# A graph layer with a routed feed-forward network: two first-layer blocks in one PSUM bank, ScalarE's copies and the result sums later in the order, and a new list of expert steps

## Chip, cores and metric

The kernel runs on one core of a Trainium2 chip. The metric is the device time of one execution in microseconds. The profile is of one further execution on the same kind of core.

## What is computed

6250 nodes have 256 features each. There are 106,250 edges (50,000 random pairs in both directions, and a loop at each node), sorted by their destination.

```python
deg = maximum(number of edges into each node, 1);  norm = deg ** -0.5
h   = layernorm(x) @ W.T + b                       # 256 -> 256
x   = x + norm * segment_sum((norm * h)[src], dst) # 6250 nodes
n   = layernorm(x)
s   = n @ Wg.T + bg                                # 8 experts
the two best experts of each node, weights p = softmax(their scores)
x   = x + sum over both: p * (relu(n @ W1[e].T + b1[e]) @ W2[e].T + b2[e])   # 256 -> 1024 -> 256
```

## The kernel before

**Preparation.** A first part (`in_order`, up to line 320) counts the edges of each node, normalises the rows and writes them as a table to HBM, each as two float16 halves.

**Chunks.** The edges are cut into 831 chunks of 128. The main loop (line 840) runs over the chunks as slots `s`. In each slot GpSimd gathers the 128 source rows of a chunk by an indirect DMA, six slots ahead (`gather`, line 387, into 24 `rows` buffers), VectorE makes a 0/1 matrix of destinations (`mask`), and one matmul on TensorE adds the rows up by destination (`add_up`, line 399) in a PSUM tile `ps`. A window of destinations closes every few chunks: `join` (line 470) adds the high and low halves on VectorE into `rolled`, and ScalarE copies 32 to 96 rows of it into `whole`, the sums of a tile of 128 nodes (line 486).

**Node tiles.** There are 49. `FINAL[t]` is the last chunk that adds to tile t. From the slot after it on, a fixed order of small parts follows: `turn_sum` transposes the sums, `linear` multiplies by W and Wg, `route` (one part in each slot) does the layer norm, picks the two experts, finds each row's place in its experts' queues (a small matmul "rank", `pp`), sorts the rows by expert through `sort` (matmuls with a 0/1 matrix) and `send` writes them by eight DMAs into the queues in HBM (`hq`, from `ordered`). ScalarE takes part with copies out of PSUM and the exponential `ex`.

**Expert steps.** A step takes up to 256 rows (or 128) of one expert's queue, the fullest one, which the chip itself finds (`choose`). `load_first`, `load_rows` and `load_second` issue the DMAs of W1, of the rows `xT` and of W2 on SP's queue. The arithmetic of a step is cut into pieces. `up(step, b)` (line 722) is one first-layer block: 128 of the 1024 hidden units, four float32 matmul instructions into a PSUM tile `ph`, then a Relu by ScalarE into `hid` (line 732). There are eight. `down(step, i)` (line 734) is two of the eight parts of the second layer for 128 rows: four matmul instructions into `py`; after every fourth piece VectorE adds the bias (`y`, line 744) and SP writes 128 rows to `yq`. A step of 256 rows has 8 + 8 pieces, one of 128 rows 8 + 4.

**The order around the change.** All of it is written out in Python; each engine runs its instructions in that order. `tasks[s]` has what a slot runs beside its chunk. Steps follow tiles: one step for each tile from tile 3 on, two for tiles 42, 44 and 46 (`FOLLOWS`). `fetch` (choice and loads) starts 14 slots after the tile's last chunk, the first piece 14 slots later (`earliest`). Each slot runs one piece, and a second in every fourth slot when the next step is due too (lines 848 to 850). In the slots behind the last chunk (`ftail`) one piece runs in each slot, steps are chosen and loaded as they are used up, and the results are read back by indirect DMAs (`read_back`), added to x by VectorE (`add_in`) and stored. There are 56 steps: 49 from the list and 7 behind it, the last four of 128 rows, so 13,824 rows. `DONE` lists pairs of a step and a number of tiles: once that step is done the results of so many tiles are taken to be there. If the chip finds that one was not, or another assumption failed, it sets `bad` and runs a second, general program (`any_order`).

[...] `ps`, `ph` and `py` have two buffers each, `pt` and `px` one.

Of the kernel before, what the change touches and what calls it, by code (L numbers as in the profile page):

```python
# [7 lines left out]
F32 = mybir.dt.float32  # L8
# [11 lines left out]
P = 128  # L20
N = 6250
NT = 49
# [14 lines left out]
SLOTS = 64  # L37
FIRST_STEP = 3
EXTRA = (42, 44, 46)
FOLLOWS = [t for t in range(FIRST_STEP, NT) for _ in range(1 + (t in EXTRA))]  # L40
USUAL = len(FOLLOWS) + 7
SHORT = 4
W1C = 2 * H + HB
# [14 lines left out]

DONE = ((40, 29), (42, 33), (43, 34), (44, 35), (45, 36), (46, 38), (47, 39), (48, 40), (49, 41), (50, 42),
        (51, 44), (52, 45), (53, 46), (54, 47), (USUAL - 1, NT))  # L60
LATER = 1 << 17
# [71 lines left out]
def in_order(ctx: ExitStack, tc: tile.TileContext, g: Shared):  # L133
# [7 lines left out]

    yq = dram.tile([P + USUAL * FT, D], F32, name="fyq")

# [207 lines left out]
    for step, t1 in DONE:  # L351
        nc.vector.memset(bounds[:, t0:t1, :], float(P + (step + 1) * FT))
        t0 = t1
# [19 lines left out]
    nc.vector.memset(most, 0.0)  # L373

    zero = keep.tile([P, FT * D // P], F32, name="zero")
    nc.gpsimd.memset(zero, 0.0)  # L376

# [5 lines left out]
    def free_order(ins, others, why):  # L383
        for o in others:
            tc.declare_no_dep(ins.ins, o.ins, reason=why)
# [63 lines left out]

    def clear_results():  # L450

        for step in range(USUAL - SHORT, USUAL):
            r0 = P + step * FT + P
            nc.sync.dma_start(yq[r0:r0 + FT - P, :], zero[:, :D])

    kept = {w: (WINDOWS[w - 1][0] % P, WINDOWS[w][0] - WINDOWS[w - 1][0]) for w in range(1, len(WINDOWS))}
    keeps = {}
    for j, key in enumerate(sorted(set(kept.values()))):  # L460
        keeps[key] = keep.tile([P, 1], F32, name=f"keep{j}")
        nc.gpsimd.memset(keeps[key], 1.0)  # L462
        for t, p0, p1 in pieces(key[0], key[0] + key[1]):
            nc.gpsimd.memset(keeps[key][p0:p1, :], 0.0)
    whole, turned_sums, turned_inputs = {}, {}, {}

# [3 lines left out]
    def join(w):  # L470

        nonlocal rolled
        n0 = WINDOWS[w][0]
        n1 = WINDOWS[w + 1][0] if w + 1 < len(WINDOWS) else NP
        ps = sums.pop(w)
        new = work.tile([P, D], F32, name="rolled", bufs=3)
        if w:
            nc.vector.scalar_tensor_tensor(new, rolled, keeps[kept[w]], ps[:, 0:D], op0=OP.mult, op1=OP.add)  # L478
        else:
            nc.vector.tensor_copy(new, ps[:, 0:D])  # L480
        nc.vector.tensor_add(new, ps[:, D:2 * D], new)  # L481
        rolled = new
        for t, p0, p1 in pieces(n0, n1):
            if p0 == 0:
                whole[t] = work.tile([P, D], F32, name="whole")
            nc.scalar.activation(whole[t][p0:p1, :], new[p0:p1, :], AF.Copy)  # L486
# [158 lines left out]

    def rows_of(step):
        return P if USUAL - SHORT <= step < USUAL else FT

    def choose(step):
        n = rows_of(step)  # L650
        seen = placed
# [32 lines left out]
        to = work.tile([P, 1], F32, name="to")  # L684
        nc.vector.tensor_scalar(to, of[:, 0:1], -1.0, float(P + step * FT - LATER), op0=OP.mult, op1=OP.add)
        mine = work.tile([P, NT, 2], F32, name="mine")
# [10 lines left out]
    def load_rows(step):  # L697

        f = steps[step]
        assert sent >= f["known"]  # L700
        col = nc.values_load(f["go"][0:1, 1:2], engines=(SP,), min_val=0, max_val=CAP - FT)
        f["xT"] = work.tile([P, FT, 2], F32, name="xT", bufs=4)
        n = rows_of(step)
        nc.sync.dma_start(f["xT"][:, :n, :], hq[bass.ds(f["we"], P), bass.ds(col, n), :])
# [6 lines left out]
    def fetch(step):  # L711

        for _ in choose(step):
            yield
            if step in steps and "w1" not in steps[step]:
                load_first(step)
        while sent < steps[step]["known"]:
            yield
        load_rows(step)
        load_second(step)  # L720

    def up(step, b):
        f = steps[step]
        w1 = f["w1"]
        n = rows_of(step)
        if b == 0:
            f["hid"] = work.tile([P, HB, FT], F32, name="hid")
        ph = psp.tile([P, FT], F32, name="ph")
        for k in range(2):
            nc.tensor.matmul(ph[:, :n], w1[:, k * H + b * P:k * H + (b + 1) * P], f["xT"][:, :n, k],  # L730
                             start=(k == 0), stop=(k == 1))
        nc.scalar.activation(f["hid"][:, b, :n], ph[:, :n], AF.Relu, bias=w1[:, 2 * H + b:2 * H + b + 1])  # L732

    def down(step, i):
        f = steps[step]
        a = i // 4
        if i % 4 == 0:
            f["py"] = psp.tile([P, D], F32, name="py")
        for b in (2 * (i % 4), 2 * (i % 4) + 1):
            nc.tensor.matmul(f["py"], f["hid"][:, b, a * P:(a + 1) * P], f["w2"][:, b * D:(b + 1) * D],  # L740
                             start=(b == 0), stop=(b == HB - 1))
        if i % 4 == 3:
            y = work.tile([P, D], F32, name="y", bufs=4)
            nc.vector.tensor_add(y, f["py"], f["w2"][:, HB * D:])  # L744
            r0 = P + step * FT + a * P
            w = nc.sync.dma_start(yq[r0:r0 + P, :], y)
            free_order(w, reads, "results are written once, and read once written")
            writes.append((step, w))
        if i == 4 * rows_of(step) // P - 1:
            del steps[step]  # L750


# [16 lines left out]

    earliest = {}  # L770
    for t in range(NT):
        s = FINAL[t] + 1
        plan_at(s + 2, turn_sum, t)
        plan_at(s + 4, linear, t)
        in_parts(s + 5, route, t)
        s += LATE[t]
        for i, step in enumerate(k for k, tile in enumerate(FOLLOWS) if tile == t):
            in_parts(s + 14 + 4 * i, fetch, step)
            earliest[step] = s + 28 + 4 * i
    for w, (n0, chunks) in enumerate(WINDOWS):  # L780
        tasks.setdefault(chunks[-1] + 1, []).insert(0, (join, (w,)))
    plan_at(3, centre)
    for t in range(0, NT, 2):
        plan_at(4 + t // 2 * 3, inputs_turned, t, min(t + 2, NT))
        plan_at(6 + t // 2 * 3, inputs_scored, t, min(t + 2, NT))
    plan_at(30, clear_results)
    chosen = loaded1 = loaded2 = len(FOLLOWS)
    all_sent = FINAL[NT - 1] + 1 + 19

    cur = 0  # L790
    done = 0

# [4 lines left out]

    def read_back(pool, where, t, j, upto=USUAL - 1):
        yb = pool.tile([P, D], F32, name="yb", bufs=12)
        r = nc.gpsimd.indirect_dma_start(  # L800
            out=yb, out_offset=None, in_=yq[0:P + (upto + 1) * FT, :],
            in_offset=bass.IndirectOffsetOnAxis(ap=where[:, t, j:j + 1], axis=0))
        free_order(r, [w for step, w in writes if step > upto], "rows of later steps aren't read")
        reads.append(r)
        return t, j, yb
# [5 lines left out]
    def store(t0, t1, engine=None):  # L811
# [4 lines left out]
        if t1 == NT:  # L816
            engine.dma_start(g.out[(NT - 1) * P:N, :], g.xr[:LAST, NT - 1, :])

    def next_piece(s):

        nonlocal cur, done
        step = done
        if step >= USUAL or "xT" not in steps.get(step, {}) or s < earliest.get(step, 0):
            return
        if cur < HB:
            up(step, cur)
        else:
            down(step, cur - HB)
        cur += 1
        if cur == HB + 4 * rows_of(step) // P:  # L830
            done += 1
            cur = 0

    with tc.manual_schedule():
        with rowp as rowpool:
            for c in range(AHEAD):
                gather(c)
            for c in range(MASKS):
                mask(c)
            for s in range(NC):  # L840
                if s + AHEAD < NC:
                    gather(s + AHEAD)
                if s + MASKS < NC:
                    mask(s + MASKS)
                add_up(s)
                for fn, args in tasks.pop(s, []):
                    fn(*args)
                next_piece(s)
                if s % 4 == 0 and earliest.get(done + 1, NC) <= s:
                    next_piece(s)  # L850
        with tc.tile_pool(name="ftail", bufs=2) as pool:
# [16 lines left out]
            while done < USUAL or tasks or len(plan) > 1 or asked < 2 * allowed or pend:  # L868
                for fn, args in tasks.pop(s, []):
                    fn(*args)  # L870
                if s > all_sent:
                    if chosen < min(USUAL, done + 4):
                        run(choose(chosen))
                        chosen += 1
                    if loaded2 < min(loaded1, done + 3):
                        load_second(loaded2)
                        loaded2 += 1
# [8 lines left out]
                if len(plan) > 1 and done > plan[0][0] and s >= since.get(plan[0][0], 0) + 6 \  # L886
                        and asked == 2 * allowed:
                    step, t1 = plan.pop(0)
                    results(allowed, t1, float(P + (step + 1) * FT))
                    allowed = t1  # L890
# [10 lines left out]

            results(allowed, NT, float(P + USUAL * FT))
            late = work.tile([P, NT, 2], F32, name="late", bufs=1)
# [555 lines left out]
```

## Time and profile before

| | |
|---|---|
| median of 3 runs | 1585.66 us (1575.81, 1585.66, 1592.05) |
| profiled execution | 1341.47 us, its span 1339.7 us |
| mean granted TensorE clock in it | 0.956 |
| busy share: TensorE, VectorE, GpSimd, ScalarE | 88%, 74%, 67%, 30% |
| gathers (GpSimd, line 389) | 831, 953 ns each |
| first-layer matmuls (line 730) | 1792 |
| second-layer matmuls (line 740) | 1728 |
| Relu (line 732) | 448, 465 ns each |
| HBM | 269.01 MB read, 55.42 MB written |

The profile comes from one execution, which was shorter than the three timed ones. A group of instructions is named by its line, engine, and output and inputs; "idle before" is the time in which its engine did nothing before it, with what ended that wait. A matmul's recorded duration runs to the modelled end of its pipeline, so successive matmuls overlap in the record, and their starts tell the rate. "PEld" is the loading of weights into TensorE. SP's DMA issues and register loads are not counted as busy.

### The profile page before, as it was taken

The page shows a single profiled execution, that of the slowest core. Times are in us where ns is not written, and L with a number is a line of the kernel's source. Part 1 is how long each engine was busy: PE and PEld are TensorE (multiplying, and loading weights), DVE is VectorE, ACT ScalarE, POOL GpSimd, SP SyncE. Part 2 cuts the span into 40 slices and gives each one's busy share as a digit, 9 for nine tenths or more (in the row PEclk, how much of TensorE's full clock was granted, in tenths as well). Part 3 has the DMA queues.
Part 4 walks back from the last instruction along what each step waited for, and adds up shares of the span by engine and source line. Part 5 has one row for each costly group of instructions (what it writes and reads, how often), then busy time and mean ns, then how long its engine had stood idle before and what let it go on. Part 6 is the DMA issues. An engine that isn't in the chain of part 4 may idle for free.

```text
span 1339.7 us, 23956 instructions
## 1 busy us (share of the span) xinstructions
PE 1179.6 (88%) x6224; PEld 901.0 (67%) x6224; DVE 985.5 (74%) x5327; ACT 402.5 (30%) x931; POOL 903.7 (67%) x984
## 2 busy tenths in 40 slices
PE   4439895999899999999999999999999999889984
PEld 4417562777576677767777676776777777678873
DVE  8842657787888888888888888888877775765542
ACT  2622331232333233332323323233232222222221
POOL 2047777777777777777777777777777775347743
PEclk9999666999999999999999999999999999799987
DMA  8353456788787878788787888877978987679882
GB/s 297 112 160 104 122 138 193 227 282 272 230 250 261 274 239 286 239 268 265 251 289 228 279 258 254 288 240 270 296 229 280 296 305 236 230 235 338 313 314 89
DMA packets 158459, 326.16 MB, mean 243 GB/s; under 512 B 26708, under 2 KB 105256, under 8 KB 143976
## 3 DMA queue, kind: packets, MB, share of 16 engines
q1 hardware_dynamic: 110780, 194.17, 42.1%
q0 software_dynamic: 46864, 129.82, 33.2%
q8 instruction: 51, 0.84, 0.3%
q14 instruction: 96, 0.79, 0.2%
q10 hardware_dynamic: 668, 0.55, 0.1%
HBM read 269.01 MB, written 55.42 MB: 242 GB/s over the span
## 4 chain that ended last, share of the span: by engine, by line
PE 46%; DMA 23%; DVE 16%; issue 5%; SPq 5%; ACT 4%; POOL 2%; POOLq 0%; ACTq 0%; DVEq 0%
PE ph L730 18%; PE py L740 11%; DMA xT<-fhq 8%; PE ps L403 7%; DMA fhq<-ordered 6%; SPq L641 4%; DMA yb<-fyq,rowat 4%; DMA rows<-ftable,src 3%; PE ph L446 2%; PE pt L501 2%; PE px L629 2%; DVE mask L396 2%; DVE y L744 1%; POOL yb L800 1%; DVE rolled L481 1%
## 5 line engine op out<-in xcount | busy, mean ns | idle before, releaser
L389 POOL DMA_INDIRECT rows<-ftable,src x831 | 791.6, 953 | 253.1 <-issue 105.5
L730 PE MATMUL ph<-xT,w 128*128 128x256 f32 (+1 forms) x1792 | 472.4, 392 | 45.4 <-DMA xT<-fhq 35.7
L740 PE MATMUL py<-w,hid 128*128 128x256 f32 x1728 | 435.8, 382 | 3.9 <-DVE y L744 3.9
L730 PEld LDWEIGHTS ph<-xT,w 128*128 128x128 f32 x1792 | 322.5, 192 | 144.8 <-issue 46.6
L740 PEld LDWEIGHTS py<-w,hid 128*128 128x128 f32 x1728 | 329.8, 192 | 80.4 <-DVE y L744 4.1
L403 PE MATMUL ps<-rows,mask 128*128 128x512 f16 x831 | 318.6, 399 | 38.0 <-DMA fyq<-zero 29.9
L732 ACT ACTIVATE hid<-ph,w 128x256 f32<-128x256 f32 (+1 forms) x448 | 204.6, 465 | 291.5 <-PE ph L730 283.8
L396 DVE TENSOR_SCALAR mask<-col_b,rel 128x128 f16<-128x128 bf16 x831 | 210.0, 272 | 28.9 <-PE ps L403 28.8
L486 ACT ACTIVATE whole<-rolled 32x256 f32<-32x256 f32 (+2 forms) x156 | 64.6, 414 | 346.2 <-DVE rolled L481 345.5
L800 POOL DMA_INDIRECT yb<-fyq,rowat x98 | 94.1, 960 | 90.4 <-DVE mx L543 26.2
L403 PEld LDWEIGHTS <-mask 128*128 128x128 f16 x831 | 87.4, 105 | 67.3 <-POOL keep L462 26.1
L744 DVE TENSOR_TENSOR y<-py,w 128x256 f32<-128x256 f32 x108 | 45.4, 421 | 96.2 <-PE py L740 93.3
L478 DVE SCALAR_TENSOR_TENSOR rolled<-rolled,keep,ps 128x256 f32<-128x256 f32 x149 | 70.7, 474 | 18.0 <-PE ps L403 17.6
L808 DVE SCALAR_TENSOR_TENSOR xr<-yb,prob,xr 128x256 f32<-128x256 f32 x98 | 45.7, 482 | 50.7 <-DMA yb<-fyq,rowat 49.6
L481 DVE TENSOR_TENSOR rolled<-ps,rolled 128x256 f32<-128x256 f32 x150 | 63.6, 424 | 5.2
L501 PE MATMUL pt<-gw,uT 128*128 128x264 f32 x196 | 55.9, 411 | 2.0 <-DVE spot L595 2.0
L509 DVE SCALAR_TENSOR_TENSOR xr<-pt,norm,xr 128x256 f32<-128x256 f32 x49 | 23.7, 483 | 41.7 <-PE pt L501 41.5
L446 PEld LDWEIGHTS ph<-wg,turned 128*128 128x128 f32 x196 | 38.6, 289 | 16.8 <-ACT turned L438 16.1
L199 PE MATMUL count<-oh,ol 128*16 128x8 bf16 (+2 forms) x898 | 28.9, 174 | 22.2 <-DVE oh L188 17.9
L501 PEld LDWEIGHTS pt<-gw,uT 128*128 128x128 f32 x196 | 39.4, 203 | 13.5 <-DVE spot L595 2.1
L376 POOL MEMSET zero<- 128x512 f32 x1 | 0.5, 524 | 64.5 <-DMA ftable<-tab 64.5
L199 PEld LDWEIGHTS <-ol 128*16 128x16 bf16 x898 | 28.7, 109 | 22.5 <-DVE ol L185 16.2
(188 smaller groups left out, 1144.6 us busy)
## 6 DMA issues: line engine op xcount, KB each, us to landing
w<-in_W SPq DMA_DIRECT2D x56, 1152.0 KB
w<-in_W SPq DMA_DIRECT2D x56, 1028.0 KB
fhq<-ordered SPq DMA_DIRECT2D x392, 64.0 KB
fyq<-y SPq DMA_DIRECT2D x108, 128.0 KB
xT<-fhq SPq DMA_DIRECT2D x52, 256.0 KB
rows<-ftable,src POOLq DMA_INDIRECT x831
out<-xr POOLq DMA_DIRECT2D x11, 512.0 KB
xr<-in_x SPq DMA_DIRECT2D x6, 896.0 KB
```

The source lines that it names most:

```text
L389: nc.gpsimd.indirect_dma_start(out=rows[c], out_offset=None, in_=table[:, :], in_offset=bass.IndirectOffsetOnAxis(ap=g.src[:, c:c + 1], ax ...
L396: nc.vector.tensor_scalar(masks[c], g.col_b[:, r:r + P], g.rel[:, c:c + 1], None, op0=OP.is_equal)
L403: nc.tensor.matmul(sums[w], masks.pop(c), rows.pop(c), start=(c == chunks[0]), stop=(c == chunks[-1]))
L446: nc.tensor.matmul(px, xT[:, k, (t - t0) * P:(t - t0 + 1) * P], wg[:, k, :], start=(k == 0), stop=(k == 1))
L478: nc.vector.scalar_tensor_tensor(new, rolled, keeps[kept[w]], ps[:, 0:D], op0=OP.mult, op1=OP.add)
L481: nc.vector.tensor_add(new, ps[:, D:2 * D], new)
L486: nc.scalar.activation(whole[t][p0:p1, :], new[p0:p1, :], AF.Copy)
L501: nc.tensor.matmul(pl, uT[:, k, :], gw[:, k, :], start=(k == 0), stop=(k == 1))
L730: nc.tensor.matmul(ph[:, :n], w1[:, k * H + b * P:k * H + (b + 1) * P], f["xT"][:, :n, k], start=(k == 0), stop=(k == 1))
L732: nc.scalar.activation(f["hid"][:, b, :n], ph[:, :n], AF.Relu, bias=w1[:, 2 * H + b:2 * H + b + 1])
L740: nc.tensor.matmul(f["py"], f["hid"][:, b, a * P:(a + 1) * P], f["w2"][:, b * D:(b + 1) * D], start=(b == 0), stop=(b == HB - 1))
L800: r = nc.gpsimd.indirect_dma_start(out=yb, out_offset=None, in_=yq[0:P + (upto + 1) * FT, :], in_offset=bass.IndirectOffsetOnAxis(ap=where ...
```

## The change

1. `ph` becomes `[P, 2, 256]` float32, 2 KB in each partition. Blocks b = 0 and 1 of a step share one buffer, 2 and 3 the next, and so on; the number of buffers stays two.
2. ScalarE's copies of `rolled` into `whole` leave `join` and become a task of their own, `part_of`, two slots later (`BEHIND = 2`); all that follows a tile's last chunk moves by two slots as well.
3. The addition of the bias and the write of `y` leave `down` and become a task of the next slot, `leave`, which counts finished steps in `gone`.
4. The steps no longer follow tiles. `STREAM` lists for 49 steps the slot in which `fetch` starts (from 136 to 841) and the number of rows; seven of them have 128. `TAIL` lists nine more. This makes 58 steps and 13,568 rows. The first piece of a listed step comes 14 slots after its fetch at the earliest (`LEAD`). `START` has the first row of each step in `yq`.
5. The number of pieces in a slot follows from a credit: 1250 a slot, less 222 for the chunk and the listed costs of tile tasks, capped at 2000; a piece costs 915 or 870 (600 for a first-layer block of 128 rows), and pieces run while the credit is above zero and the step's loads have been issued.
6. `fetch` puts off W1 until fewer than three steps lie ahead, and W2 by the same rule on `gone`.
7. `DONE` has new pairs; `clear_results` (four DMAs of zeros) and its tile `zero` go.

```diff
-            in_parts(s + 14 + 4 * i, fetch, step)
-            earliest[step] = s + 28 + 4 * i
+    for step, (s, n) in enumerate(STREAM):
+        in_parts(s, fetch, step)
+        earliest[step] = s + LEAD
...
+STREAM = ((136, 256), (150, 256), (162, 256), (169, 256), (180, 256), (205, 256), (215, 256), (228, 128),
...
+          (841, 128))
+TAIL = (256, 256, 256, 256, 256, 256, 128, 128, 128)
+LEAD = 14
+BEHIND = 2
+SLOT = 1250
+CHUNK = 222
+SPARE = 2000
+TASKS = dict(turn_sum=220, linear=890, rank=100, sort=430, inputs_turned=800, inputs_scored=1570)
+PIECES = {FT: (915, 870), P: (600, 870)}
...
         if b == 0:
             f["hid"] = work.tile([P, HB, FT], F32, name="hid")
-        ph = psp.tile([P, FT], F32, name="ph")
+        if b % 2 == 0:
+            f["ph"] = psp.tile([P, 2, FT], F32, name="ph")
+        ph = f["ph"][:, b % 2]
...
         if i % 4 == 3:
-            y = work.tile([P, D], F32, name="y", bufs=4)
-            nc.vector.tensor_add(y, f["py"], f["w2"][:, HB * D:])
-            r0 = P + step * FT + a * P
-            w = nc.sync.dma_start(yq[r0:r0 + P, :], y)
...
+            plan_at(s + 1, leave, step, a, f["py"], f["w2"])
...
+    def leave(step, a, py, w2):
+
+        nonlocal gone
+        y = work.tile([P, D], F32, name="y", bufs=4)
+        nc.vector.tensor_add(y, py, w2[:, HB * D:])
+        r0 = START[step] + a * P
+        w = nc.sync.dma_start(yq[r0:r0 + P, :], y)
...
+        if a == ROWS_OF[step] // P - 1:
+            gone += 1
...
-        s = FINAL[t] + 1
+        s = FINAL[t] + 1 + BEHIND
...
         tasks.setdefault(chunks[-1] + 1, []).insert(0, (join, (w,)))
+        plan_at(chunks[-1] + 1 + BEHIND, part_of, w)
...
-                next_piece(s)
-                if s % 4 == 0 and earliest.get(done + 1, NC) <= s:
+                credit = min(credit + SLOT - CHUNK - busy.get(s, 0), SPARE)
+                while credit > 0 and ready(s):
+                    credit -= PIECES[ROWS_OF[done]][cur >= HB]
                     next_piece(s)
```

## The prediction

> **What bounds the kernel now.** I read the page first, then the table by stages, the gather's tile, the timeline of a few first-layer blocks, and the waits.
>
> ```profile
> span 1339.7 us, 23956 instructions
> ...
> PE 1179.6 (88%) x6224; PEld 901.0 (67%) x6224; DVE 985.5 (74%) x5327; ACT 402.5 (30%) x931; POOL 903.7 (67%) x984
> ...
> POOL 2047777777777777777777777777777775347743
> PEclk9999666999999999999999999999999999799987
> ```
>
> TensorE looks like the bound at 88%, POOL like a bystander at 67%. Neither is so. The next view has the gathers between 276 and 1140 us, then the stages (columns: length, busy time of the five engines, granted clock, DMA).
>
> ```profile
> L389 POOL DMA_INDIRECT rows<-ftable,src x678: 942/946/1189, 275.3 to 1127.3; - x170
> its engine sat idle before it (us, times) until:
> issue: 81.9, 268
> PE ps L403: 48.7, 160
> ```
>
> ```profile
> 82.00:276.00 194.00, 158.09 (x672) 114.01 (x673) 109.22 (x604) 49.86 (x137) 147.12 (x169) 0.82 0.57 165
> 276.00:1148.00 872.00, 830.23 (x3848) 622.55 (x3848) 706.43 (x4031) 272.21 (x636) 645.70 (x678) 0.99 0.81 261
> 1148.00:1340.00 192.00, 159.62 (x738) 133.36 (x736) 103.50 (x482) 44.88 (x104) 102.95 (x109) 0.90 0.77 263
> ```
>
> Gathers start every (1127.3 - 275.3) / 677 = 1.258 us: 0.95 us each and 0.30 us of idle time between, always 0.30, whoever is named (48.7 / 160). So while chunks last, from 82 to 1127 us, POOL sets the pace, one chunk in 1.258 us, and TensorE has to fit its work of a chunk into that. Behind the last chunk (its matmul ends at 1148 us) TensorE and the end of the results set the time: 192 us.
>
> What TensorE needs is read from starts, since its busy time counts each matmul to its modelled end.
>
> ```profile
> 1184.27 3.54 PE L730 MATMUL ph<-xT,w 128*128 128x256 f32 x15
> ...
> 1185.37 0.47 ACT L732 ACTIVATE hid<-ph,w 128x256 f32<-128x256 f32 x1 [4.50 <-PE ph L730]
> 1186.27 0.47 ACT L732 ACTIVATE hid<-ph,w 128x256 f32<-128x256 f32 x1 [0.43 <-PE ph L730]
> ```
>
> Fifteen matmuls in 3.54 us, the last of 0.387 us, start every 0.225 us, so a first-layer block of 256 rows (4 matmuls) takes 0.90 us. The Relu of each block (1185.37, 1186.27) runs while the matmuls of the next block go on without a gap. That is what the change touches.
>
> Other spacings, from the same timeline: second-layer matmul 0.216 (a piece of 4: 0.864), chunk 0.215, and per node tile 1.59 (four linear at 0.222, four sorts and two transposes at 0.109, the rank). From slot 103 to 830 the planner puts 702 pieces (352 blocks, 350 second-layer pieces), 728 chunks and 43 tiles: 318 + 302 + 157 + 68 = 846 us, or 1.162 us a slot, against 1.258 from POOL. TensorE has 8% to spare.
>
> **What the Trainium skill says.** "PSUM — Partial Sum Buffer", section on bank collisions: two engines must not use one bank within one 32-partition quadrant at the same time, also at different columns, and the guard has to go by bank, not by address. The trace agrees as far as it can: today each block has a bank of its own (8 in all), and Relu and the next block overlap. "TensorE: Matmul & The Clock Gate", Part 1: after an idle window of some 3.4 us the clock drops to half, and a busy window brings it back. The trace shows 0.5 from 1101.9 to 1105.3 after a lull, and 0.82 on average between 82 and 276 us. "ScalarE: Activation LUTs", on what an ACTIVATE costs: 280 ns + 0.833 ns an element with a bias operand, 493 ns for 256; the trace has 0.47, which I use.
>
> **The change part by part.**
>
> *Two blocks in one bank.* The tile is [P, 2, 256] float32, exactly a bank. The order is: matmuls of block 0, Relu 0, matmuls of block 1 into the other half, Relu 1. By the rule above the matmuls of every odd block must wait until the Relu of the even one has left the bank. Even blocks find the other bank free. Price of such a wait: natural start of the next block 1184.27 + 4 x 0.225 = 1185.17; Relu ends 1185.37 + 0.47 = 1185.84; difference 0.67. Waking, from the nearest row:
>
> ```profile
> 700.71 0.84 ACT L732 ACTIVATE hid<-ph,w 128x256 f32<-128x256 f32 x2
> ...
> 701.24 1.17 PE L730 MATMUL ph<-xT,w 128*128 128x256 f32 x4 [0.89 <-ACT hid L732]
> ```
>
> The first of two Relus ends near 701.18, TensorE starts 0.05 later, and four matmuls take 1.17 instead of 3 x 0.225 + 0.387 = 1.06, since the weights weren't loaded ahead: 0.11 more. Together 0.83 us. For 128 rows (Relu 0.367, matmul spacing 0.114) the same sum is 0.72. From it goes whatever TensorE does between the two blocks. Behind the waiting matmul stand, on TensorE's queue, the chunks and tiles that follow, and behind these POOL once its 24 row buffers are full.
>
> I followed the new planner's rules slot by slot: before slot 831 there are 183 odd blocks. 113 have only a chunk between (0.61 left), 31 have nothing (the full price), 39 have a tile's work as well (8 us in all). Sum 69 + 25 + 8 = 102 us. After slot 831 there are 25 long and 24 short ones, all back to back: 21 + 17 = 38 us.
>
> *The searched list.* Steps begin at slot 150 instead of 103, and until then TensorE has only chunks and inputs and keeps up: slot 150 is at its gather, 271.6, plus 4.8 for the landing = 276 us. From 150 to 830 come 710 pieces (334 long and 32 short blocks, 344 second-layer pieces), 681 chunks and 40 tiles: 302 + 15 + 297 + 146 + 64 = 824 us, or 1.210 a slot. That alone would still fit under 1.258 (856 us). With 102 us of waits it is 926 us and doesn't: TensorE becomes the bound. Add 12 us for Relus that stand behind another waiting ScalarE instruction (ex and h2s; 183 x 0.07, worked out from ScalarE's remaining waits). Last chunk: 276 + 926 + 12 = 1214 us against 1148: +66.
>
> *Rows.* 13568 rows instead of 13824, in 58 steps instead of 56. Behind the chunks stay 136 us of pieces against 143: -7. Two more loads of both weights are 4.4 MB, under 2% of 326 MB, hidden.
>
> *Copies and results put off.* ScalarE waits for `rolled` 345.5 us, with Relus queued behind; two chunks later the sums are there. Today this delay costs TensorE 22.9 + 8.7 us in the middle stage; the 102 us already assume a prompt Relu. DVE's result sum one slot later can fall behind a waiting `add_in` (49.6 us over 31 waits), and the last list of readable tiles reads eight rows of results late instead of two: +6 together.
>
> *Lead.* TensorE waits 24.7 us for xT in the middle stage; loads now stand 2 to 17 slots behind the last send instead of 1. Worth nothing once TensorE is late anyway. Removing the four clearing DMAs and one memset (0.5 us): nothing.
>
> *Tail.* 192 - 7 + 38 + 6 - 4 (waits that 128-row blocks have today, 16 pairs of 0.27) - 6 (half of the 7.4 us for a weight DMA and 3.9 us for y that the chain shows near 1290 us; with more TensorE time in a step they land earlier relative to it) = 219.
>
> Sum: 1214 + 219 = 1433 us span, +93 or +6.9%. With the 1.8 us around the span 1435 against 1341.47. The median of the runs, 1585.66, is 18% over the profiled execution, and no view tells why. I carry the ratio: 1585.66 x 1435 / 1341.47 = about 1695.
>
> **Rivals.**
>
> *The runs are slow because gathers are slow.* 244 us over 831 chunks is 0.29 a slot; at 1.55 a slot TensorE's 1.36 fits, the 102 us are hidden, and only the tail's +27 stays: 1612. For it: the stretch is POOL's already. Against it: POOL's pace is steady in the profile.
>
> *The runs are slow because TensorE is slower throughout.* Before, slot 103 begins at 82 + 103 x 1.258 + 5 = 216 us and the tail has 49 us beside its pieces; 216 + (846 + 143) / c + 49 = 1585 gives c = 0.75. At that clock the stream is TensorE's in both kernels, the idle slots from 103 to 150 are lost as well, and the sum is 276 + 824 / 0.75 + 114 in the stream and 136 / 0.75 + 38 + 40 in the tail: 1748.
>
> *The pair doesn't wait,* faster: Relu and the matmuls of the other half overlap. Place: each odd block; it decides if TensorE's slot stays under 1.258. Then the stream ends at POOL's pace near 1138, the tail loses 7 + 4 and keeps the rest, 181: 1319, -1.6%, 1561. For it: the slot sum of 1.210. Against it: the bank rule.
>
> *The change doesn't do what it says:* a step finishes later than the new `DONE` list allows, and the kernel runs its other program as well. At least 831 x 1.258 = 1045 us more: beyond 2600. Nothing in the profile shows it.
>
> **How the numbers follow.** Forecast 0.64, slow gathers 0.12, slow TensorE 0.12, no wait 0.10, fallback 0.02. The range 1600 to 1760 takes in the first three and leaves the last two out. A measurement here tells about 1% from no change (the runs shown spread by 1%). Faster takes 0.08 of the no-wait case, same its rest and 0.03 of slow gathers, slower the remainder.
>
> **What would show it.** PE `ph` waiting on ACT `hid` near 100 to 140 us instead of 34 (25.5 + 8.7); matmuls of L730 in groups of four with a gap behind every first block of a pair; gathers with idle times above 0.30 us that end on `ps`; last chunk near 1214. Wrong, if the first-layer blocks still run back to back, or if the gathers keep 1.258 us to the end.

## The result, and the profile after

| | before | after |
|---|---|---|
| median of the runs | 1586.04 us (4 runs, 1575.81 to 1592.05) | 1675.55 us (4 runs, 1670.44 to 1682.45) |
| ratio | | 1.0574, 95% interval 1.0507 to 1.0641 |
| profiled execution | 1341.47 us | 1670.44 us |

The change makes the kernel 5.7% slower: +89.5 us. The forecast was 1695 us.

Before's runs in this table took 18% longer than its profiled execution and than its runs beside all experiments but the last (about 1340 us), and after's took 14% longer than in e5, so a time is set only against the runs of before beside it. After's profile here shows where the time goes; the sum of the prediction is held against e5 below.

The page of after, with the lines that answer to those of before:

```profile
span 1668.7 us, 24140 instructions
...
PE 1255.9 (75%) x6256; PEld 914.8 (55%) x6256; DVE 997.7 (60%) x5377; ACT 404.7 (24%) x947; POOL 900.7 (54%) x983
...
POOL 1076666556565655555565646565665564246613
PEclk9999666589998989999998989999999999889898
```

POOL has the same 901 us of work as before and is less dense: slices of 5 and 6 where before had 7s. TensorE's share fell from 88% to 75% although it executes 32 matmuls more. Neither engine is saturated, so something holds them. The gathers between the first slot with an expert piece (150) and the last:

```profile
L401 POOL DMA_INDIRECT rows<-ftable,src x661: 940/946/1180, 340.7 to 1402.1; - x166
its engine sat idle before it (us, times) until:
PE ps L415: 223.4, 172
issue: 125.1, 394
```

One gather still takes 0.946 us, as before; they start every (1402.1 - 340.7) / 660 = 1.61 us instead of 1.258, and what ends half of the idle time (223.4 of some 435 us) is TensorE's chunk matmul, which gives a row buffer back. POOL waits for TensorE now. The stages (length, busy time of the five engines, granted clock, DMA):

```profile
82.00:341.00 259.00, 143.86 (x556) 92.85 (x557) 104.02 (x573) 42.69 (x122) 162.96 (x186) 0.74 0.38 110
341.00:1434.00 1093.00, 913.22 (x3997) 658.77 (x3996) 721.82 (x4087) 282.15 (x663) 626.94 (x661) 0.95 0.66 214
1434.00:1669.00 235.00, 167.16 (x738) 132.10 (x736) 105.47 (x504) 44.29 (x107) 103.35 (x109) 0.88 0.63 216
```

The clock is 0.95 in the long stage, so a TensorE that is slow throughout is not the reason. From the list of waits, by engine and line (sum in us, times, longest):

```profile
POOL rows L401 <- PE ps L415: 262.1, 194, 10.5
PEld ph L747 <- ACT hid L749: 199.3, 136, 6.9
...
PE ph L747 <- ACT hid L749: 138.8, 122, 6.4
```

The first-layer matmuls of `ph` wait for the Relu `hid` in the 100 to 140 us that the prediction named. In before the same line has:

```profile
PE ph L730 <- ACT hid L732: 8.7, 11, 1.9
```

The wait of PEld is the same wait seen from the weight loads (they run ahead of the matmuls and idle longer); the two are not added, as the prediction did for its 34 us (25.5 of PEld and 8.7). After's trace holds only 1397 of the semaphore events that TensorE's instructions raise, where e5's holds 2001, so its list of waits has gaps. The list of e5 is the safer one.

### The profile page after: what moved, and what is told of

Same layout as the page of the kernel before. It is cut to its first block, busy times and chain, and to the rows that moved or that the text cites. A ratio compares the mean times of both kernels' runs of the same rounds, so it can differ in the third digit from the quotient of the medians.

```text
span 1668.7 us, 24140 instructions
## 1 busy us (share of the span) xinstructions
PE 1255.9 (75%) x6256; PEld 914.8 (55%) x6256; DVE 997.7 (60%) x5377; ACT 404.7 (24%) x947; POOL 900.7 (54%) x983
## 4 chain that ended last, share of the span: by engine, by line
PE 58%; DVE 15%; issue 11%; ACT 7%; another core or an unknown queue 6%; DMA 1%; ACTq 1%; POOL 1%; DVEq 0%; POOLq 0%
PE ph L747 24%; PE py L757 16%; PE ps L415 9%; ACT hid L749 4%; PE pt L512 2%; PE ph L458 2%; PE px L640 1%; DVE mask L408 1%; PE px L447 1%; DVE rolled L482 1%; DVE rs L543 1%; PE count L214 1%; PE pt L503 1%; ACT whole L497 1%
## 5 line engine op out<-in xcount | busy, mean ns | idle before, releaser
L747 PE MATMUL ph<-xT,w 128*128 128x256 f32 (+1 forms) x1856 | 511.9, 406 | 204.3 <-ACT hid L749 138.8
L747 PEld LDWEIGHTS ph<-xT,w 128*128 128x128 f32 x1856 | 341.0, 204 | 360.3 <-ACT hid L749 199.3
L757 PE MATMUL py<-w,hid 128*128 128x256 f32 x1696 | 425.2, 383 | 0.0
L415 PE MATMUL ps<-rows,mask 128*128 128x512 f16 x831 | 330.3, 417 | 41.7 <-DMA rows<-ftable,src 31.3
L757 PEld LDWEIGHTS py<-w,hid 128*128 128x128 f32 x1696 | 320.7, 192 | 65.5 <-issue 0.3
L640 PE MATMUL px<-slots,h2s 128*128 128x256 f16 x196 | 32.8, 295 | 54.0 <-DVE slots L618 34.5
L641 ACT ACTIVATE ordered<-px 128x512 f32<-128x512 f32 x49 | 30.7, 627 | 161.7 <-PE px L640 66.5
L458 PE MATMUL ph<-wg,turned 128*128 128x8 f32 x196 | 40.0, 333 | 32.2 <-ACT turned L450 27.8
L588 DVE TENSOR_TENSOR h2s<-h,h2s 128x256 f16<-128x256 f32 x49 | 20.7, 423 | 65.3 <-ACT h2s L583 53.3
L640 PEld LDWEIGHTS <-h2s 128*128 128x128 f16 x196 | 19.8, 102 | 71.0 <-issue 44.6
## 6 DMA issues: line engine op xcount, KB each, us to landing
w<-in_W SPq DMA_DIRECT2D x58, 1152.0 KB
```

What stands on the lines that cost most here:

```text
L415: nc.tensor.matmul(sums[w], masks.pop(c), rows.pop(c), start=(c == chunks[0]), stop=(c == chunks[-1]))
L458: nc.tensor.matmul(px, xT[:, k, (t - t0) * P:(t - t0 + 1) * P], wg[:, k, :], start=(k == 0), stop=(k == 1))
L640: nc.tensor.matmul(px[:, k, :], h2s[t][:, i, k * P:(k + 1) * P], slots[t], start=(i == 0), stop=(i == 1))
```

## The experiments

In all experiments but the last, before took 1340.33 us beside e1 to e4, 1339.54 beside e5 to e8 and 1339.35 beside e9 to e11. These agree to 0.1%, so runs of these three sets (e5 and e4, say) are also set against each other. "Dead time" below is worked out from the trace: the distance between the starts of successive matmuls less the usual spacing of that shape (0.225 us for `ph`, 0.216 for `py`, 0.215 for a chunk and so on).

**e1, before once more.** No edit.

> The kernel before, unchanged, with a new profile: its profiled execution (1341 us) was 15% shorter than its timed ones (1586 us), while the changed kernel's profiled execution (1670 us) is among its timed ones. If the two kernels were profiled under different conditions, this profile has a span near 1580 us and shows where the 240 us lie: slow gathers (POOL's pace near 1.5 us all along, TensorE not late), or a TensorE that is held up (gathers idle over 0.30 us on ps). If the profile is always shorter than the timed runs, it is near 1341 us again.

Measured: 1337.72 us, span 1335.9, with gathers every 1.258 us and the last chunk at 1145.6 us. A profiled execution isn't shorter by nature: the whole set around it took about 1340 us, timed runs included. So the 18% belongs to the set of runs, not to the profiler.

**e5, after once more.** No edit; the kernel that the forecast's sum of 1433 us was made for.

> The changed kernel, unchanged, beside the other experiments (there the kernel before takes 1340 us). Pair theory with the measured parts: one bank to a block took 1372, and pairs added 134 us to the kernel before, so 1372 + 100 to 145 = 1470 to 1515 us, 10 to 13% over the kernel before. If the list of steps absorbs the waits (its slots have room where the old order has none), nearer to 1433, the span of the forecast.

Measured: 1465.64 us against 1339.54, ratio 1.0939 (1.0913 to 1.0964), +126 us, where the forecast had +93. Its stages:

```profile
277.00:1252.00 975.00, 883.58 (x3996) 642.25 (x3996) 718.73 (x4079) 284.28 (x663) 643.19 (x677) 0.99 0.75 241
1252.00:1465.00 213.00, 159.89 (x739) 127.57 (x737) 105.68 (x504) 44.65 (x108) 103.24 (x109) 0.92 0.69 239
```

Slot 150 comes at 277 us (forecast 276), the last chunk at 1252 (forecast 1214), the tail is 213 us (forecast 219). TensorE's waits for the Relus:

```profile
PE ph L747 <- ACT hid L749: 110.0, 199, 3.6
```

The price of the wait can be read in the tail, where blocks stand back to back. The timeline (start, duration, engine and line, what it is; in brackets the idle time before it and what ended it):

```profile
1331.67 2.08 PE L747 MATMUL ph<-xT,w 128*128 128x256 f32 x8 [0.56 <-ACT hid L749]
...
1332.88 0.47 ACT L749 ACTIVATE hid<-ph,w 128x256 f32<-128x256 f32 x1 [1.26 <-PE ph L747]
...
1333.78 0.47 ACT L749 ACTIVATE hid<-ph,w 128x256 f32<-128x256 f32 x1 [0.43 <-PE ph L747]
1334.31 2.08 PE L747 MATMUL ph<-xT,w 128*128 128x256 f32 x8 [0.56 <-ACT hid L749]
```

A group of eight matmuls is an odd block and the even one of the next pair, which finds the other bank free. Then comes a stop for the Relu. Pairs start every 1334.31 - 1331.67 = 2.64 us; two blocks of 0.90 leave 0.84, the forecast's 0.83. Counted over all odd blocks of 256 rows back to back, the median is a dead time of 0.725 plus a slower restart of 0.106 (the weights aren't loaded ahead); behind one chunk it is 0.511 + 0.106 = 0.62; for 128 rows 0.619 + 0.106 = 0.73. The forecast had 0.83, 0.61 and 0.72.

What it had too small is the Relu that comes late. In the middle of the stream:

```profile
815.57 1.07 PE L747 MATMUL ph<-xT,w 128*128 128x256 f32 x4
...
818.95 0.20 ACT L575 ACTIVATE ex<-ex 128x1 f32<-128x1 f32 x1 [6.67 <-DVE ex L574]
819.06 0.46 ACT L749 ACTIVATE hid<-ph,w 128x256 f32<-128x256 f32 x1
819.56 0.97 PEld L747 LDWEIGHTS ph<-xT,w 128*128 128x128 f32 x4 [3.22 <-ACT hid L749]
819.57 1.70 PE L747 MATMUL ph<-xT,w 128*128 128x256 f32 x4 [2.71 <-ACT hid L749]
```

The even block's matmuls are done by 816.64, but its Relu stands on ScalarE's queue behind the exponential `ex` of a tile, which has waited 6.67 us for VectorE. The Relu starts at 819.06, and TensorE, which stands on the next block, waits 2.71 us. Thirteen such stops of over 1 us lie in the stream.

**e3, only the shared bank, in the kernel before.**

```diff
-        ph = psp.tile([P, FT], F32, name="ph")
+        if b % 2 == 0:
+            f["ph"] = psp.tile([P, 2, FT], F32, name="ph")
+        ph = f["ph"][:, b % 2]
```

> The kernel before with one thing done: two first-layer blocks in one bank, order and list of steps as before. Pair theory: 224 odd blocks wait 0.4 to 0.8 us each, 90 to 180 us of TensorE time, so 1670 to 1760 us. Rival (the list costs the time): within 2% of 1586.

Measured: 1474.12 us, ratio 1.0993 (1.0968 to 1.1018), +134 us; last chunk at 1258.8. Its waits:

```profile
PEld ph L732 <- ACT hid L734: 228.2, 217, 3.7
PE ph L732 <- ACT hid L734: 140.9, 200, 3.0
```

The few lines of the tile alone cost as much as the whole change (+126), and a little more: beside them, the rest of the change adds nothing. What the rest costs without them is in the next run.

**e2, the change without the shared bank.** `ph` is again one tile of a block; list, pieces and the things put off stay.

```diff
-        if b % 2 == 0:
-            f["ph"] = psp.tile([P, 2, FT], F32, name="ph")
-        ph = f["ph"][:, b % 2]
+        ph = psp.tile([P, FT], F32, name="ph")
```

> The changed kernel with one thing undone: each first-layer block has a bank of its own again (two buffers). Pair theory (odd blocks wait for the even block's Relu, and that is what the change costs): the median 0.62 us in front of odd blocks goes, waits of PE ph on ACT hid fall from 139 us (PE) to under 40, and the time falls by 100 to 200 us, to 1480 to 1580, at or below the kernel before. Rival (the new list of steps and the tasks put off cost the time, pair waits are hidden under others): it stays within 2% of 1675.

Measured: 1371.68 us, ratio 1.0237 (1.0220 to 1.0254). 94 of the 126 us are gone, but 31 are left, where the no-wait case had a gain of 1.6%. The waits that remain:

```profile
PE px L640 <- DVE slots L618: 32.1, 18, 4.6
PE ph L745 <- ACT hid L747: 25.2, 18, 2.8
```

**e4, the bank shared, the two Relus behind the matmuls of both blocks.**

```diff
-        nc.scalar.activation(f["hid"][:, b, :n], ph[:, :n], AF.Relu, bias=w1[:, 2 * H + b:2 * H + b + 1])
+        if b % 2:
+            for c in (b - 1, b):
+                nc.scalar.activation(f["hid"][:, c, :n], f["ph"][:, c % 2, :n], AF.Relu,
+                                     bias=w1[:, 2 * H + c:2 * H + c + 1])
```

> The changed kernel with the Relu of an even block put behind the matmuls of its odd partner: matmuls 0, matmuls 1, Relu 0, Relu 1, in the same shared bank, so four blocks are in flight and nothing waits inside a pair. Pair theory (it is the order within a bank, not the bank itself): like the kernel with one block to a bank or faster, 1450 to 1570 us. Rival (sharing a bank slows matmuls or Relus as such): stays near 1675.

Measured: 1355.32 us, ratio 1.0110 (1.0082 to 1.0139); last chunk at 1164.7. Waits, and the timeline of a few blocks:

```profile
PE px L640 <- DVE slots L618: 51.9, 30, 4.6
...
PE ph L747 <- ACT hid L751: 6.6, 6, 2.1
```

```profile
1245.16 7.38 PE L747 MATMUL ph<-xT,w 128*128 128x256 f32 x32
1247.22 0.84 ACT L751 ACTIVATE hid<-ph,w 128x256 f32<-128x256 f32 x2 [8.25 <-issue]
1248.97 0.84 ACT L751 ACTIVATE hid<-ph,w 128x256 f32<-128x256 f32 x2 [0.91 <-PE ph L747]
```

With the same shared bank, all 32 matmuls of a step run through without a stop, and the Relus come in twos. So it isn't the sharing that costs, but reading one half before the other is written. It even beats a bank for each block (e2) by 16 us: two buffers of two blocks let TensorE run up to four blocks ahead of a late Relu, and its waits for `hid` fall from 25.2 us (e2) to 6.6. Whether the wait guards the bank or the tile no run tells, since the two halves are one bank and one tile at once.

**e6, the same two edits in the kernel before.**

> The kernel before with two blocks in one bank, but both blocks' matmuls ahead of both Relus; list and order as before. Pair theory (only the order inside a bank matters, four blocks in flight help a little): 1325 to 1340 us. If sharing a bank costs anything as such: above 1345.

Measured: 1334.12 us, ratio 0.9963 (0.9949 to 0.9977). PE's waits of `ph` for `hid`, 4.6 us beside 18.9 for PEld in e1, are no longer listed. Against this kernel the new list with all that belongs to it (e4) costs 21 us. The next runs ask where these lie.

**e7, e4 with the copies not put off** (`BEHIND = 0`, which also puts all that follows a tile's last chunk two slots earlier).

> The changed kernel with both blocks' matmuls ahead of both Relus (1355 us), and ScalarE's copies and the tiles' tasks not put off (0 instead of 2 slots). In its stream TensorE waits 35 us for the sort's 0/1 matrix, which VectorE makes. If that wait comes from where the two slots put a tile's tasks among VectorE's other work, it falls under 10 us and the time to 1320 to 1335. If it comes from a TensorE that is filled to the brim by the list, it stays, and the time is 1350 to 1370, with more waits for Relus behind the copies.

Measured: 1353.77 us, ratio 1.0118 (1.0096 to 1.0140): the same as e4. The copies' place is worth nothing either way.

**e8, e4 with the result sum at once.**

```diff
-            plan_at(s + 1, leave, step, a, f["py"], f["w2"])
+            leave(step, a, f["py"], f["w2"])
```

> The changed kernel with both blocks' matmuls ahead of both Relus (1355 us), and the result sum not put off: VectorE adds the bias in the slot of the last second-layer piece, ahead of the next slot's tasks. If the result sum at the head of a slot is what makes VectorE late for the sort (35 us of waits), those fall under 15 us and the time to 1325 to 1340. Otherwise within 0.5% of 1355.

Measured: 1376.18 us, ratio 1.0269 (1.0249 to 1.0290). The sign is the other way round: putting it off gains 21 us. VectorE's wait for the last second-layer matmul, first in e8, then in e4:

```profile
DVE y L772 <- PE py L760: 69.1, 42, 5.1
```

```profile
DVE y L772 <- PE py L760: 32.1, 24, 4.4
```

VectorE runs its instructions in the order written. While it stands on `y`, the layer norm, the masks and the 0/1 matrix `slots` behind it stand too. The dead time of TensorE in the stream goes from 65 us (e4) to 84 us (e8), 19 of the 21 us. That the stops on `y` are what TensorE then waits for is argued, not shown: its dead time in front of the sort's matmuls grows by only some 8 us (35 to 43), and the rest is spread over many tiles.

**e9, e6 with the steps begun later.** `FIRST_STEP = 6` and `EXTRA = (12, 18, 24, 42, 44, 46)`: as many steps over fewer slots, as the new list does by starting at slot 150.

> The kernel before with both blocks' matmuls ahead of both Relus (1334 us), and the expert steps begun late: the first follows tile 6 instead of tile 3 (slot 153 instead of 103), and three tiles (12, 18, 24) get a second step, so that as many pieces as before are done when the chunks end. Late-start theory (the new list's own cost is that TensorE idles in slots 103 to 150 and then has no room): 846 us of pieces, chunks and tiles less the 15 us before slot 150 plus some 70 us of other waits are 900 us in 681 slots, more than POOL's 855; the last chunk moves from 1145 to 1165 to 1185 us and the time to 1355 to 1370. Rival (the list costs through where it puts its steps and tasks, not through its start): within 0.7% of 1334.

Measured: 1341.29 us, ratio 1.0017 (0.9994 to 1.0039); last chunk 1152.0 against 1144.5 in e6. The late start explains some 7 of the 21 us, not 20 to 30.

**e10, e6 with the result sum put off by a slot** (the `leave` of the change, in the old order).

> The kernel before with both blocks' matmuls ahead of both Relus (1334 us), and the result sums put off to the next slot. In the new list this put-off was worth 21 us (1376 without, 1355 with). If it is a gain wherever TensorE waits for VectorE: 1315 to 1328. In the old order, whose stream is held by the gathers, such waits are covered: then within 0.4% of 1334.

Measured: 1330.10 us, ratio 0.9925 (0.9901 to 0.9949). Waits:

```profile
DVE y L754 <- PE py L745: 43.4, 51, 5.6
```

In e6 this line has 87.6 us over 61 waits. With e11, which takes the same within the noise, this is the fastest of the kernels here, and it beats both kernels of the comparison.

**e11, e10 with the copies put off by a slot as well.**

> The same, and ScalarE's copies of the sums put off by one slot as well (the tiles' other tasks where they were). ScalarE no longer stands in front of sums that VectorE has not made: its waits for them (345 us before) fall to under 150. If TensorE's waits for late Relus (9 to 20 us in the stream) are what is left to gain: 1320 to 1330. If the gathers hold the stream anyway: within 0.4% of 1334.

Measured: 1331.37 us, ratio 0.9938 (0.9917 to 0.9960). ScalarE waits 107.5 us for `rolled` instead of 262 in e10, and the time doesn't move. That fits two blocks in hand: in neither run does the list of waits have TensorE's `ph` standing on `hid`.

**e12, e4 with pieces spread evenly** (all costs in `TASKS` zero, `SLOT = 1155`).

> The changed kernel with both blocks' matmuls ahead of both Relus (1355 us), and the credit blind to a tile's tasks: their listed costs are zero and a slot gives 1155 instead of 1250, so the number of pieces before the last chunk stays the same (one more) but they are spread evenly. If it is the levelling of TensorE's slots that brings it to the sort before VectorE has made the 0/1 matrix (35 us of waits there), these waits fall under 15 us and the time to 1335 to 1345. If not, within 0.7% of 1355.

Measured: 1615.33 us against 1609.58 for before beside it, ratio 1.0023 (0.9996 to 1.0050). These runs were as long as those of the result, and e4 was not run among them, so the question (does the credit by free TensorE time cause the rest of the 21 us?) isn't answered. Its waits for `slots` are not smaller, but in such a set they may also hold stops like those of the last section:

```profile
PE px L640 <- DVE slots L618: 91.7, 21, 13.1
...
PE px L640 <- DVE slots L617: 23.1, 10, 4.0
```

It does show that the list without the pairs' waits costs next to nothing against before in such a set, which suggests that the +89.5 us of the result are the pairs' waits too.

## Why the prediction came out as it did

**The mechanism was right.** The wait of each odd block for the even one's Relu is the cause, by removal (e5 to e4, -110 us; e5 to e2, -94) and by addition alone (e3, +134). What the prediction took from the Trainium skill ("PSUM — Partial Sum Buffer", the section on bank collisions: the guard has to go by bank) agrees with the traces as far as they go: the block writes other columns than the Relu reads, and waits until the Relu's semaphore releases it (110.0 us in e5). They don't tell a guard by bank from one by tile. e4 adds that the order of writes and reads within the bank decides.

**The sum of the stream, term by term** (all from e5):

| term | forecast | measured |
|---|---|---|
| slot 150 | 276 | 277 |
| TensorE's work, slots 150 to 830 | 824 | 975 (277 to 1252) less 153 of dead time: 822 |
| odd blocks at the plain price | 102 | 103 |
| Relus behind another waiting ScalarE instruction | 12 | 26 |
| other waits of TensorE | 0 | 24 (half clock 9.6, `slots` 8, the rest small) |
| last chunk | 1214 | 1252 |

The plain price is 25 x 0.83 + 105 x 0.62 + 14 short ones (8) + 9 for those behind tile work = 103. All dead time at odd blocks is 129, so the late Relus are 26: that term was mis-sized. The forecast spread a mean of 0.07 us over all pairs; in fact a few stops of 2 to 3 us carry it, most of them behind `ex` (16 us of late start) and `whole` (7; in two of these `h2s`, just ahead of the copy, had waited 4 to 5 us for VectorE). The second term that failed is a missing one. The forecast let TensorE be the bound and then gave it no other waits than the pairs'. An engine without slack pays all its waits, small ones too. Half clock is one of them. The prediction took an idle window of some 3.4 us for it from the Trainium skill ("TensorE: Matmul & The Clock Gate", Part 1); the lull in before that it set beside this, ahead of 1101.9, has only 1.84 us of idle time.

**The tail** came out at 213 against 219, partly by errors that cancel. The pairs' waits are 41 us there (forecast 38). Without them the tail is 190 us (e4), not 181. But about 18 us of its other waits (dead time 37 us in e4, 60 - 41 = 19 in e5) vanish beside the pairs' waits, where the forecast let 10 go.

**"That alone would still fit under 1.258"** is the step that failed outright, and with it the no-wait rival's 1319 us. Without the pairs' waits the list takes 1355 (e4) or 1372 us (e2). 824 us of work against POOL's 856 leaves 32 us of slack, but e4 has 65 us of dead time, 35 of it the sort's matmuls, which wait for `slots`: 824 + 65 = 889, and the last chunk comes at 1165 instead of 1138. Of the 21 us between e6 and e4, the late start is some 7 (e9). Why `slots` is late so much more often in the new list (52 us against 10 in e6) wasn't settled: without the put-off copies it is still 40 us (e7), and without the put-off result sum 48 (e8). In the changed kernel as it stands most of this is hidden (8 us of dead time in e5's stream against 35 in e4's); that VectorE gains what TensorE loses at each pair would explain it, but is not tested.

**The things put off.** "+6 together" had the wrong sign, as far as it was measured: both were taken back only in kernels without the pairs' waits. The result sum's put-off is worth 21 us in the list and 4 in the old order (ratio 0.9925 against 0.9963, intervals that just touch). The forecast asked what `y` would wait behind; it left out what waits behind `y`. The copies were worth nothing (e7, e11), as the sum had it. The waits for `xT`, 24.7 us before, fell to nearly nothing (3.9 us in e4). What that is worth no run separates; the forecast put it at nothing.

**The carrying to the timed runs.** The sum said +6.9%; in the shorter runs the change costs 9.4% (1.0939), in the longer ones 5.7% (1.0574). The forecast of 1695 lies near 1675.55 because a stream that was 38 us too short met a set of runs in which the change costs less: 90 us instead of 126. That it lies so near is luck: two errors cancel. Neither of the two rivals for these runs fits after's profile: a gather takes 0.946 us there as well, and POOL waits for TensorE, not the other way round; the clock is 0.95 in the stream. For before's long runs there is no trace, but beside e12 its mean clock is 0.91 (0.96 in the short sets), not the 0.75 that the second rival needed. At 1675 us the second program (beyond 2600) did not run. Why the change costs less in such a set is open; what the trace shows of it stands in the last section.

## What to carry to other kernels

Two blocks may share a PSUM bank without waiting for each other if both are written before either is read (1466 to 1355 us here); write, read, write, read made every second block wait for the reader's end, the waking and the weight load, less the work that stands between. Such a wait can be priced to 0.01 us from two starts in the timeline, but the reader's own queue has to be looked through as well: a few late readers cost a quarter as much again here (26 us beside 103). When a change turns an engine into the bound, add to its work every wait that it has in the old trace, since there is no slack left to hide them.

## What was not expected of the hardware

In the result's set of runs VectorE and ScalarE stop for 6 to 13 us at a stretch and TensorE starts nothing for 20, while POOL goes on. The timeline of after, in the stage before the expert steps:

```profile
104.00 1.06 PE L447 MATMUL px<-ident,xr 128*128 128x128 f32 x4
...
108.19 0.18 ACT L460 ACTIVATE xg<-ph 128x8 f32<-128x8 f32 x1 [6.35 <-remote]
...
114.52 0.18 ACT L460 ACTIVATE xg<-ph 128x8 f32<-128x8 f32 x1 [6.14 <-remote]
...
116.62 0.37 DVE L408 TENSOR_SCALAR mask<-col_b,rel 128x128 f16<-128x128 bf16 x1 [13.08 <-remote]
...
125.78 0.60 ACT L450 ACTIVATE turned<-px 128x512 f32<-128x512 f32 x1 [11.08 <-remote]
...
126.42 0.38 PE L458 MATMUL ph<-wg,turned 128*128 128x8 f32 x1 [20.51 <-ACT turned L450]
```

The same place in e5, the same kernel in the shorter set:

```profile
106.03 1.06 PE L447 MATMUL px<-ident,xr 128*128 128x128 f32 x4
...
107.18 0.60 ACT L450 ACTIVATE turned<-px 128x512 f32<-128x512 f32 x1 [1.18 <-PE px L447]
```

The copy of `px` follows its matmuls by 1.2 us in e5 and by 21.8 us in after. "remote" stands where no instruction that could have released the wait ended shortly before. The packed trace tells more: all four waits end within 0.1 us of an event of the semaphore that TensorE's matmuls raise (at 108.17, 114.49, 116.59 and 125.69), while the last matmul before them is recorded as over at 105.92. So VectorE and ScalarE stand on a semaphore of TensorE that comes up to 20 us after the recorded (modelled) ends of its matmuls; the trace of e12 has the same at 109 to 127 us. Slot 150, before any pair, comes at 341 us in after and at 277 in e5, so 64 of the 204 us between the two profiled spans are lost where the change isn't at work yet. Whether the matmuls themselves or their semaphore are held back, and by what, no run here shows. The record gives chips numbered 2, 5 and 8 for the three short sets and 15 for e12, and none for the result, so a difference between chips, or what else ran beside them, is a rival that was not tested.

And one thing of size: a float32 matmul that starts from a wait, without its weights loaded ahead, is followed by the next after 0.33 us instead of 0.225, in e5 as in e3.
